# A four-layer state-space stack on one core: output scaling moved behind the projection, additions moved to identity matmuls and ScalarE copies

## The chip, the cores and the metric

The kernel runs on one core of a Trainium2 chip. The metric is the device time of one execution in microseconds (us). The engines are called PE (TensorE), DVE (VectorE), ACT (ScalarE), POOL (GpSimd) and SP (SyncE, which here issues every DMA). Each engine executes its own instructions in the order in which the program gives them, and waits at semaphores for the others.

## The reference

Eight images of 48 x 48 positions and 96 channels pass through four residual layers, `x = x + layer(groupnorm(x))`. Layers 0 and 3 are two-dimensional selective scans, layer 1 is a filtered expansion (upsampling, a polynomial, downsampling), and layer 2 is a selective scan along lines in four directions. What the change touches is the end of layers 0 and 3, and the end of layer 2:

```
# layers 0 and 3, y: sum of the four scans, 192 channels
mu = y.mean(-1); yc = y - mu; var = (yc * yc).mean(-1)
y = yc * rsqrt(var + 1e-5) * out_norm_w + out_norm_b
y = y * silu(z)
x = x + y @ out_proj_w.T                     # 192 -> 96 channels

# layer 2, one term for each direction k
x = x + (y_k * silu(z_k)) @ w_k ... + out_b
```

Everything is float32.

## The kernel before

The channels lie on the partitions and the positions along the free axis. The 192 inner channels are kept as two halves of 96. An image is cut into five blocks of positions (`BLKS`: four of 480 and one of 384).

`scans()` drives layers 0, 2 and 3. It goes over the images (jobs), the four directions and the five blocks, 160 blocks a layer. A block has four turns. A turn makes three scans on DVE (L263); each needs a pair of decays `ps_da` that ACT writes into PSUM (L255, two buffers), and products `dbu` that DVE and POOL make (L235). POOL then multiplies the scanned states by the C rows (L276), and PE sums them over the states (L296, L298). Where a block carries on from the one before it, ACT copies the carried state into `dbu` (`bring`, L243). Nothing is scheduled by a planner: the order on each engine is the order of the Python statements.

Each turn calls `aside()` twice. Such a call is a half-turn here. In this order, it loads data for the next block, advances the generator `side(job)` by one `yield`, runs a step of `stage1` (which prepares a block two blocks ahead), and runs what `later` holds. On DVE the first call of a turn falls before the third scan and the second one after it.

In layers 0 and 3 `side(job)` finishes the image before (`post`) and then prepares the next one (`front`, `conv`), beside the scans of the image in hand. For the last image `post` runs alone, after the last scan. `post` has two loops over the five blocks. The first subtracts the mean (L507), squares (L510) and sums to variances (L515). The second, in which a block takes five half-turns, is this:

- load the stored silu(z) (`zin`, one buffer) and the residual rows (`xi`, two buffers) by SP; spread the reciprocal deviations over the partitions by PE into `pr` (L534)
- DVE multiplies each half of `y` by `out_norm_w` and by `pr` (L538)
- POOL multiplies `y` by z (L541); PE starts the projection with the norm's bias, `wnb` times z (L544)
- PE adds the projection of `y` (L547)
- DVE adds the result to `xi` (L550), and SP stores it (L552) at the start of the next block's first half-turn

`pr`, `po` and all other PSUM tiles of the side work are one buffer, the tag "side". In `stage1` of these layers PE's projection `s0` (L593) stands in slot 0 of a block's eight half-turns, and ACT's copy of it (`bcl`, L598) in slot 1; `raw` (L583) on PE stands in slots 3 and 4, and `biased` (L587) on ACT in slots 4 and 5. These run after the side work of the same half-turn.

In layer 2 (`lines`) `done()` hands over a finished block: DVE multiplies by the gate (L785), one half-turn later `project()` lets PE project it into a PSUM tile of tag "s1" (two buffers, L794), and another half-turn later `add()` lets DVE add it to the image `xs` in place (L800 for direction 0, with the bias `l2_outb`; L802 for the others). For two directions the positions are taken by columns, so that the image is read and written with a step of 48 elements.

Of the kernel before, what the change touches and what calls it, by code (L numbers as in the profile page):

```python
# [9 lines left out]
F32 = mybir.dt.float32  # L10
AF = mybir.ActivationFunctionType
ALU = mybir.AluOpType
# [3 lines left out]
H, W, C = 48, 48, 96  # L16
L = H * W
DH = 96
# [7 lines left out]
BMAX = 480  # L26
# [49 lines left out]
def vss_stack_kernel(ctx: ExitStack, tc: tile.TileContext, i: dict, out: bass.AP):  # L76
    nc = tc.nc
# [19 lines left out]
    wc = weights(const, ("gmat", "ident", "red"))  # L97
# [332 lines left out]
    def ss2d(l, xin, xout, b0=0):  # L430
# [65 lines left out]
        def post(b):  # L496
            y = yss[b]
            var = small.tile([CH, L // CH], F32, tag="var", name="var")
            for r0, nr in BLKS:
                n = nr * SEG  # L500
                s = slice(r0 * W, r0 * W + n)
# [7 lines left out]
                sq = lnp.tile([DH, 2, BMAX], F32, tag="sq", name="sq", bufs=1)  # L509
# [14 lines left out]
            for r0, nr in BLKS:  # L524
                n = nr * SEG
                s = slice(r0 * W, r0 * W + n)
                z = lnp.tile([DH, 2, BMAX], F32, tag="zin", name="zin", bufs=1)
                nc.sync.dma_start(z[:, :, :n], zs[b][:, :, s])  # L528
                xi = xio.tile([C, BMAX], F32, tag="xi", name="xi")
                nc.sync.dma_start(xi[:, :n], xin[b][:, s])  # L530
                pr = side_psum()
                for c in range(n // CH):
                    at = r0 * W // CH + c
                    nc.tensor.matmul(pr[:DH, c * CH:(c + 1) * CH], lhsT=var[:, at:at + 1].to_broadcast([CH, DH]),  # L534
                                     rhs=wc["ident"], start=True, stop=True)
                yield
# [4 lines left out]
                nc.gpsimd.tensor_mul(y[:, :, s], y[:, :, s], z[:, :, :n])  # L541
                po = side_psum()
                for half in range(2):
                    nc.tensor.matmul(po[:C, :n], lhsT=wnb[:, half, :], rhs=z[:, half, :n], start=(half == 0), stop=False)  # L544
                yield
                for half in range(2):
                    nc.tensor.matmul(po[:C, :n], lhsT=w[f"{l}_out"][:, half, :], rhs=y[:, half, s],  # L547
                                     start=False, stop=(half == 1))
                yield
                nc.vector.tensor_add(xi[:, :n], xi[:, :n], po[:C, :n])  # L550
                yield
                nc.sync.dma_start(xout[b][:, s], xi[:, :n])  # L552

        def side(job):
# [82 lines left out]
        dirs = DIRS_SS  # L637
# [11 lines left out]
    def lines(xin, xout):  # L649
# [40 lines left out]
        xs = {}  # L690
# [90 lines left out]
        def done(b, half, y):  # L781
            n = b.n
            if half == 0:
                gated[b] = gp.tile([DH, 2, BMAX], F32, tag="gated", name="gated")
            nc.vector.tensor_mul(gated[b][:, half, :n], b.zb[:, half, :n], y[:DH, :n])  # L785
            if half == 0:
                return []
            got = {}

            def project():  # L790
                got["o"] = ps("s1", 2)
                t = gated.pop(b)
                for h in range(2):
                    nc.tensor.matmul(got["o"][:C, :n], lhsT=wo[:, b.k, h, :], rhs=t[:, h, :n], start=(h == 0), stop=(h == 1))  # L794

            def add():
                xv = seq(xs[b.job], dirs[b.k][0])[:, b.r0:b.r0 + b.nr, :]
                v = rows(got["o"][:C], n)
                if b.k == 0:
                    nc.vector.scalar_tensor_tensor(xv, v, w["l2_outb"], xv, ALU.add, ALU.add)  # L800
# [17 lines left out]
        dirs = DIRS_L2  # L818
# [293 lines left out]
```

## Time and profile before

| | us |
|---|---|
| median of 3 runs | 19549.3 (19545.86 to 19551.5) |
| profiled execution, its own time | 19542.61 |
| span of the profiled execution, first to last instruction | 19540.6 |

| engine | busy us | share of the span |
|---|---|---|
| DVE | 16831.8 | 86% |
| POOL | 16028.7 | 82% |
| PE | 15237.1 | 78% |
| ACT | 14144.5 | 72% |

From the start of the span to about 6008 us layer 0 runs, to about 7230 us layer 1, to about 13540 us layer 2, and then layer 3. The mean granted PE clock is 0.744 of full speed. A float32 matmul stands in the profile as two matmul instructions, so a count of x320 is 160 matmuls.

In a row of the timeline, the first number is the start in us from the start of the span, the second the length in us, then come the engine, the line, the operation, the tile written and the tiles read, and the shape. What stands in square brackets is the idle time of the engine just before, and who ended it. In a row of a group, the busy time and the mean in nanoseconds follow the first bar, and the idle time before the instructions the second.

### The profile page before, as it was taken

How to read it: one execution, taken by the hardware profiler on the slowest of the kernel's cores; microseconds unless marked ns; L12 is line 12 of the kernel's file. 1: busy time of each engine (PE TensorE's matmuls, PEld its weight loads, DVE VectorE, ACT ScalarE, POOL GpSimd, SP SyncE). 2: the span in 40 equal slices, each digit the busy share in tenths (PEclk: the TensorE clock that was granted, in tenths of full speed). 3: DMA queues.
4: the chain of work that ended last, by engine and by line, in shares of the span. 5: the costliest groups of instructions: out<-in, count | busy, mean ns of one | idle time of the engine just before them, and what ended most of it. 6: DMA issues, size and time to landing. Idle time of an engine off the chain costs nothing. (4 is left out here: it accounts for less than half of the span.)

```text
span 19540.6 us, 172984 instructions
## 1 busy us (share of the span) xinstructions
PE 15237.1 (78%) x53500; PEld 4370.8 (22%) x53500; DVE 16831.8 (86%) x11281; ACT 14144.5 (72%) x22222; POOL 16028.7 (82%) x9825
## 2 busy tenths in 40 slices
PE   6777777777767887888888988887677777777776
PEld 1211211211214552222222222222121121121121
DVE  6999999999992228999999999996999999999997
ACT  5877777877772227788788777885778778778775
POOL 6999999999991007888888888886999999999997
PEclk6777776776767777888878888887677677667765
DMA  3444444444443324434434444443444444444443
GB/s 130 160 162 158 162 160 163 158 163 158 156 170 48 50 45 145 145 141 150 150 139 147 147 146 145 144 149 112 158 163 160 159 164 157 160 162 161 156 165 123
DMA packets 768486, 2829.44 MB, mean 145 GB/s; under 512 B 235724, under 2 KB 298668, under 8 KB 640926
## 3 DMA queue, kind: packets, MB, share of 16 engines
q1 hardware_dynamic: 767558, 2818.38, 43.1%
q8 instruction: 422, 6.91, 0.1%
q14 instruction: 506, 4.15, 0.1%
HBM read 2371.42 MB, written 446.69 MB: 144 GB/s over the span
## 5 line engine op out<-in xcount | busy, mean ns | idle before, releaser
L263 DVE TENSOR_TENSOR_SCAN dbu<-ps_da,dbu 128x962 f32<-128x962 f32 (+3 forms) x5760 | 11858.2, 2071 | 897.9 <-ACT ps_da L255 895.7
L276 POOL TENSOR_TENSOR dbu<-dbu,bc 128x1440 f32<-128x1440 f32 (+1 forms) x3840 | 11439.8, 2985 | 1040.6 <-DVE dbu L263 814.0
L255 ACT ACTIVATE ps_da<-dd,w_l_a 128x481 f32<-128x481 f32 (+3 forms) x11520 | 7414.7, 648 | 2729.7 <-DVE dbu L263 2523.7
L296 PE MATMUL ps_y<-dbu,w_red 128*32 128x480 f32 (+1 forms) x23040 | 4983.6, 752 | 3051.0 <-POOL dbu L276 3047.3
L298 PE MATMUL ps_y<-dbu,w_red 128*32 128x480 f32 (+1 forms) x7680 | 4942.9, 752 | 0.0
L235 DVE TENSOR_TENSOR dbu<-dd,ps_b 128x1440 f32<-128x1440 f32 (+5 forms) x3840 | 4645.3, 1210 | 320.1 <-ACT ps_b L216 275.7
L235 POOL TENSOR_TENSOR dbu<-dd,bc 128x480 f32<-128x480 f32 (+3 forms) x1920 | 3026.2, 1576 | 61.9 <-DMA bc<-bcd 36.6
L296 PEld LDWEIGHTS ps_y<-dbu,w_red 128*32 128x32 f32 x23040 | 742.7, 125 | 7009.7 <-POOL dbu L276 5283.6
L216 ACT COPY ps_b<-bc 128x480 f32<-128x480 f32 (+1 forms) x3360 | 1798.4, 535 | 300.7 <-DVE dbu L235 271.3
L722 PE MATMUL ps_s<-xpad,w_l_cw 128*128 128x480 f32 (+1 forms) x2560 | 1747.2, 834 | 2.3 <-ACT xpad L124 1.6
L481 PE MATMUL ps_side<-xpad,w_l_cw 128*128 128x480 f32 (+1 forms) x2880 | 1617.4, 690 | 4.6 <-ACT xpad L124 4.5
L255 ACT ACT_TABLE_LOAD x970 | 1244.5, 1283 | 17.1
L113 POOL MEMSET w_l_cw<- 128x1760 f32 (+1 forms) x3 | 5.8, 1942 | 1326.7 <-DVE x L932 1321.3
L422 POOL TENSOR_TENSOR dds<-dds,u 96x480 f32<-96x480 f32 (+1 forms) x640 | 793.6, 1240 | 259.9 <-ACT dds L611 259.9
L593 PE MATMUL ps_s<-u,w_l_xp 96*38 96x480 f32 (+1 forms) x1280 | 957.2, 888 | 4.1 <-ACT dds L587 3.0
L583 PE MATMUL ps_s<-bcl,dtw 6*96 6x480 f32 (+1 forms) x1280 | 878.4, 775 | 86.3 <-ACT dds L587 82.2
L270 POOL COPY carry<-dbu 128x3 f32<-128x3 f32 x2048 | 386.4, 189 | 582.6 <-DVE dbu L263 570.2
L292 PE MATMUL ps_y<-ysum,w_ident 96*96 96x480 f32 (+1 forms) x960 | 740.7, 861 | 113.7 <-ACT ysum L634 112.8
L481 PEld LDWEIGHTS ps_side<-xpad,w_l_cw 128*128 128x128 f32 x2880 | 571.0, 222 | 1115.0 <-issue 916.4
L722 PEld LDWEIGHTS ps_s<-xpad,w_l_cw 128*128 128x128 f32 x2560 | 525.8, 210 | 1087.1 <-issue 938.1
L298 PEld LDWEIGHTS ps_y<-dbu,w_red 128*32 128x32 f32 x7680 | 683.1, 125 | 0.0
L763 PE MATMUL ps_s<-xpad,w_l_inz 96*96 96x480 f32 (+1 forms) x640 | 505.7, 924 | 86.9 <-ACT dds L757 69.2
(146 smaller groups left out, 12586.2 us busy)
## 6 DMA issues: line engine op xcount, KB each, us to landing
dd<-dd SPq DMA_DIRECT2D x512, 1443.0 KB
bc<-bcd SPq DMA_DIRECT2D x1536, 480.0 KB
dd<-dd SPq DMA_DIRECT2D x256, 1440.0 KB
dd<-dds SPq DMA_DIRECT2D x512, 360.8 KB
dd<-dd SPq DMA_DIRECT2D x128, 1155.0 KB
bc<-bcd SPq DMA_DIRECT2D x384, 384.0 KB
dd<-dds SPq DMA_DIRECT2D x256, 360.0 KB
dd<-dd SPq DMA_DIRECT2D x64, 1152.0 KB
```

The costliest lines, as they stand in the source:

```text
L216: nc.scalar.copy(bps[t][:, :b.n], bcs[t][:, 0, :b.n])
L235: engine.tensor_mul(o, du, by.unsqueeze(1).to_broadcast([P, hi - lo, b.n]))
L255: nc.scalar.activation(da[:, at:at + b.m], b.got[half][:, u % 3, 0, :], AF.Exp, scale=a[:, b.k, ci:ci + 1])
L263: nc.vector.tensor_tensor_scan(db, da, db, 0.0, ALU.mult, ALU.add)
L276: nc.gpsimd.tensor_mul(h, h, bcs.pop(2 * t + sub)[:, 1, :n].unsqueeze(1).to_broadcast([P, 3, n]))
L296: nc.tensor.matmul(y[32 * g:32 * g + 32, :n], lhsT=wc["red"][:, :32], rhs=hc[:, g, b.at], start=False, stop=(slot == 3))
L298: nc.tensor.matmul(y[DH:, :n], lhsT=wc["red"][:, 32:], rhs=hc[:, 2, b.at], start=(slot == 0), stop=(slot == 3))
L422: nc.gpsimd.tensor_mul(rows(du, n), rows(dt, n), u)
L481: nc.tensor.matmul(pu[:, :n], lhsT=flat[:, at:at + P], rhs=xpad[:, r0 + dy:r0 + dy + nr, dx:dx + W], start=(tap == 0), stop=(tap == 8))
L583: nc.tensor.matmul(got["p"][:DH, :n], lhsT=dtw[2 * NS:, b.k, half, :], rhs=b.bcl[2 * NS:, :n], start=True, stop=True)
L593: nc.tensor.matmul(got["p"][:NBC, :n], lhsT=w[f"{l}_xp"][:, b.k, half, :], rhs=u[:, half], start=(half == 0), stop=(half == 1))
L722: nc.tensor.matmul(got["u", half][:, :n], lhsT=flat[:, at:at + P], rhs=shifted(off), start=(tap == 0), stop=(tap == 3))
```

## The change

In layers 0 and 3 the weight `out_norm_w` is multiplied into the output projection's weights once, ahead of the loops. (The product of `out_norm_b` with the same weights, `wnb`, is made from the weights as they were.) The reciprocal deviation, which is the same for all channels of a position, is applied behind the projection. So POOL's multiplication of `y` by z moves ahead of it, into the half-turn in which z is loaded. ACT copies `pr` into SBUF, PE projects `y * z`, DVE multiplies the 96 projected channels by the copy, and PE gathers the result in a second PSUM tile: the residual rows and the scaled product by two products with the identity matrix, and the bias term by its two products with z. ACT copies the sum into `xi`. The copy and the store now stand in the half-turn after these four matmuls, which is the first one of the next block.

In layer 2 `project()` begins with a product of the identity and the image's own rows, and `add()` becomes a copy on ACT (with the bias for direction 0) in place of the addition on DVE.

```diff
         for half in range(2):
             nc.scalar.activation(wnb[:, half, :], w[f"{l}_out"][:, half, :], AF.Identity, scale=w[f"{l}_nb"][:, half:half + 1])
+            wo = w[f"{l}_out"][:, half, :]
+            nc.scalar.activation(wo, wo, AF.Identity, scale=w[f"{l}_nw"][:, half:half + 1])
...
                     nc.tensor.matmul(pr[:DH, c * CH:(c + 1) * CH], lhsT=var[:, at:at + 1].to_broadcast([CH, DH]),
                                      rhs=wc["ident"], start=True, stop=True)
-                yield
-                for half in range(2):
-                    nc.vector.scalar_tensor_tensor(y[:, half, s], y[:, half, s], w[f"{l}_nw"][:, half:half + 1], pr[:DH, :n],
-                                                   ALU.mult, ALU.mult)
-                yield
                 nc.gpsimd.tensor_mul(y[:, :, s], y[:, :, s], z[:, :, :n])
+                yield
+                t = lnp.tile([DH, 2, BMAX], F32, tag="sq", name="normed", bufs=1)[:, 0, :n]
+                nc.scalar.copy(t, pr[:DH, :n])
+                yield
                 po = side_psum()
                 for half in range(2):
-                    nc.tensor.matmul(po[:C, :n], lhsT=wnb[:, half, :], rhs=z[:, half, :n], start=(half == 0), stop=False)
-                yield
+                    nc.tensor.matmul(po[:C, :n], lhsT=w[f"{l}_out"][:, half, :], rhs=y[:, half, s],
+                                     start=(half == 0), stop=(half == 1))
+                yield
+                nc.vector.tensor_mul(t, t, po[:C, :n])
+                yield
+                po = side_psum()
+                nc.tensor.matmul(po[:C, :n], lhsT=wc["ident"], rhs=xi[:, :n], start=True, stop=False)
                 for half in range(2):
-                    nc.tensor.matmul(po[:C, :n], lhsT=w[f"{l}_out"][:, half, :], rhs=y[:, half, s],
-                                     start=False, stop=(half == 1))
-                yield
-                nc.vector.tensor_add(xi[:, :n], xi[:, :n], po[:C, :n])
-                yield
+                    nc.tensor.matmul(po[:C, :n], lhsT=wnb[:, half, :], rhs=z[:, half, :n], start=False, stop=False)
+                nc.tensor.matmul(po[:C, :n], lhsT=wc["ident"], rhs=t, start=False, stop=True)
+                yield
+                nc.scalar.copy(xi[:, :n], po[:C, :n])
                 nc.sync.dma_start(xout[b][:, s], xi[:, :n])
...
+            xv = seq(xs[b.job], dirs[b.k][0])[:, b.r0:b.r0 + b.nr, :]
             def project():
                 got["o"] = ps("s1", 2)
                 t = gated.pop(b)
+                nc.tensor.matmul(got["o"][:C, :n], lhsT=wc["ident"], rhs=xv, start=True, stop=False)
                 for h in range(2):
-                    nc.tensor.matmul(got["o"][:C, :n], lhsT=wo[:, b.k, h, :], rhs=t[:, h, :n], start=(h == 0), stop=(h == 1))
+                    nc.tensor.matmul(got["o"][:C, :n], lhsT=wo[:, b.k, h, :], rhs=t[:, h, :n], start=False, stop=(h == 1))
             def add():
-                xv = seq(xs[b.job], dirs[b.k][0])[:, b.r0:b.r0 + b.nr, :]
                 v = rows(got["o"][:C], n)
                 if b.k == 0:
-                    nc.vector.scalar_tensor_tensor(xv, v, w["l2_outb"], xv, ALU.add, ALU.add)
+                    nc.scalar.activation(xv, v, AF.Identity, bias=w["l2_outb"])
                 else:
-                    nc.vector.tensor_add(xv, xv, v)
+                    nc.scalar.copy(xv, v)
```

More of the change, by code (lines that the diff above doesn't have):

```diff
@@ L535, in post @@
                                      rhs=wc["ident"], start=True, stop=True)
+                nc.gpsimd.tensor_mul(y[:, :, s], y[:, :, s], z[:, :, :n])
                 yield
-                for half in range(2):
-                    nc.vector.scalar_tensor_tensor(y[:, half, s], y[:, half, s], w[f"{l}_nw"][:, half:half + 1], pr[:DH, :n],
-                                                   ALU.mult, ALU.mult)
+                t = lnp.tile([DH, 2, BMAX], F32, tag="sq", name="normed", bufs=1)[:, 0, :n]
+                nc.scalar.copy(t, pr[:DH, :n])
                 yield
-                nc.gpsimd.tensor_mul(y[:, :, s], y[:, :, s], z[:, :, :n])
                 po = side_psum()
                 for half in range(2):
-                    nc.tensor.matmul(po[:C, :n], lhsT=wnb[:, half, :], rhs=z[:, half, :n], start=(half == 0), stop=False)
+                    nc.tensor.matmul(po[:C, :n], lhsT=w[f"{l}_out"][:, half, :], rhs=y[:, half, s],
+                                     start=(half == 0), stop=(half == 1))
                 yield
+                nc.vector.tensor_mul(t, t, po[:C, :n])
+                yield
+                po = side_psum()
+                nc.tensor.matmul(po[:C, :n], lhsT=wc["ident"], rhs=xi[:, :n], start=True, stop=False)
                 for half in range(2):
-                    nc.tensor.matmul(po[:C, :n], lhsT=w[f"{l}_out"][:, half, :], rhs=y[:, half, s],
-                                     start=False, stop=(half == 1))
+                    nc.tensor.matmul(po[:C, :n], lhsT=wnb[:, half, :], rhs=z[:, half, :n], start=False, stop=False)
+                nc.tensor.matmul(po[:C, :n], lhsT=wc["ident"], rhs=t, start=False, stop=True)
                 yield
-                nc.vector.tensor_add(xi[:, :n], xi[:, :n], po[:C, :n])
-                yield
+                nc.scalar.copy(xi[:, :n], po[:C, :n])
                 nc.sync.dma_start(xout[b][:, s], xi[:, :n])
```

## The prediction

> **What bounds the kernel now.** I read the page's busy shares and costliest groups first, then the busy time by stage, then the timeline of one image around each line that the change touches.
>
> ```profile
> span 19540.6 us, 172984 instructions
> PE 15237.1 (78%) x53500; PEld 4370.8 (22%) x53500; DVE 16831.8 (86%) x11281; ACT 14144.5 (72%) x22222; POOL 16028.7 (82%) x9825
> L263 DVE TENSOR_TENSOR_SCAN dbu<-ps_da,dbu 128x962 f32<-128x962 f32 (+3 forms) x5760 | 11858.2, 2071 | 897.9 <-ACT ps_da L255 895.7
> ```
>
> By stage (columns: window, its length, busy PE, PEld, DVE, ACT, POOL, granted clock, DMA share, GB/s):
>
> ```profile
> 145.00:5904.00 5759.00, 4262.70 (x14982) 1048.40 (x14986) 5430.73 (x3472) 4441.45 (x7258) 5306.44 (x3612) 0.70 0.47 160
> 5904.00:6008.00 104.00, 70.33 (x220) 35.69 (x212) 16.27 (x26) 7.40 (x8) 13.37 (x6) 0.61 0.10 28
> 7230.00:13540.00 6310.00, 5310.73 (x16532) 1425.48 (x16530) 5663.41 (x3813) 4927.42 (x7151) 5375.64 (x2567) 0.81 0.40 143
> ```
>
> In the first ss2d layer DVE is busy 94% and POOL 92%; in the line layer DVE 90%, POOL 85%, PE 84%, ACT 78%. DVE leads, but every engine is in a loop with it: a scan needs the decays (ps_da) from ACT, two buffers deep; ACT takes its copies in order and some wait for PE; PE waits for POOL's products. Freed DVE time counts only as far as the decays are ready, and a late POOL comes back round. From 5904 to 6008 no scans run: the last image's post() is a bare chain (it recurs in the last 107 us), and all that lengthens it is paid.
>
> **What the Trainium skill says.** "ScalarE: Activation LUTs", Table sets: copy and identity are in every set. Agreed: none of the trace's table loads stands on the Identity of L587 or the copies of L634, so the new copies bring none. "DMA: Bandwidth & Descriptors", Latency: about 2 us of fixed cost. Here z needs 4.4 us from issue to its use in the bare chain. "SBUF — State Buffer", Who interferes with whom: a DVE instruction with one SBUF input does not contend with GpSimd. The removed DVE operations read one from SBUF and one from PSUM, so POOL should not speed up; its 96x960 product takes 2.20 us in the bare chain with DVE idle, 2.22 among the scans: agreed. "TensorE: Matmul & The Clock Gate", HAM oscillation: PE after idle gaps runs at half clock. Agreed: two 480-column matmuls (four instructions) take 3.5 us or 1.8 us.
>
> **The change, part by part.** Call the steps of a post() block A to E, one to each half-turn, and F the end, which falls into the next block's A.
>
> *DVE.* Removed by their groups: L538 102.5, L550 50.1, L800 27.5, L802 102.5 = 282.6 us. Added: 80 products of L550's shape, 50.1. Net -232.5 us. DVE also waited for PE before these (14.9 + 110.2 + 33.1 + 82.9 = 241 us); those waits move to ACT, which now reads the results.
>
> *ACT.* 160 copies in post at 0.55 (0.47 for the short block): 85 us. 160 in the line layer: 80 in row order at 0.55 to 0.65, 80 in column order at 0.97 (L634's column rows): 125 us. Four small weight scalings: 1 us, before the loop.
>
> *PE.* 160 identity matmuls in post and 160 in lines. L544 and L547 give 428.2/320 = 1.34 us a matmul, L794 423.1/320 = 1.32: 426 us, beside other work except where named below.
>
> *Lines.* In one block (DVE, then ACT):
>
> ```profile
> 9026.64 2.15 DVE L263 TENSOR_TENSOR_SCAN dbu<-ps_da,dbu 128x960 f32<-128x960 f32 x1
> 9029.07 0.71 DVE L800 SCALAR_TENSOR_TENSOR x<-ps_s,w_l_outb,x 96x480 f32<-96x480 f32 x1 [0.28 <-PE ps_s L794]
> 9029.71 2.14 DVE L263 TENSOR_TENSOR_SCAN dbu<-ps_da,dbu 128x960 f32<-128x960 f32 x1
> ```
>
> ```profile
> 9027.86 1.36 ACT L255 ACTIVATE ps_da<-dd,w_l_a 128x480 f32<-128x480 f32 x2
> 9029.64 1.35 ACT L255 ACTIVATE ps_da<-dd,w_l_a 128x480 f32<-128x480 f32 x2
> ```
>
> Without the addition the scan of 9029.71 could start at 9029.25, when its decays are ready: gain 0.45, not 0.99. The same two limits at 159 blocks give 146 us. But ACT's copy now waits for a project() one matmul longer (mean 1.1 us there) and delays the next decays. Taking from each block's slack this wait and a copy of 0.55 or 0.95 us leaves 90 or 60 us. I take **-75 us**; ends -146 (ACT's wait costs nothing) and -20 (the longer PE queue delays decays again later).
>
> *Last post(), twice.* Before, a block takes 11.4 us (from the end of one addition, 5975.87, to the next, 5987.25); z's load covers the norm's work and is itself exposed:
>
> ```profile
> 5976.37 0.56 SPq L528 DMA_DIRECT2D zin<-zd  x1
> 5980.80 2.20 POOL L541 TENSOR_TENSOR ysum<-ysum,zin 96x960 f32<-96x960 f32 x1 [10.07 <-DMA zin<-zd]
> 5984.05 2.52 PE L547 MATMUL ps_side<-ysum,w_l_out 96*96 96x480 f32 x4
> 5986.60 0.65 DVE L550 TENSOR_TENSOR xi<-xi,ps_side 96x480 f32<-96x480 f32 x1 [7.40 <-PE ps_side L547]
> ```
>
> After: 0.5 to the issue of z, 4.4 to POOL, 2.2 product, two matmuls 2.7 (between 1.8 and 3.5), DVE product 0.7, then four matmuls 5.4 (3.7 to 7.0), which all stand behind that product because "side" has one PSUM buffer, ACT copy 0.55 and handovers 0.25: 16.7. Four intervals of 43.5 us become 64 (the last shorter), +21; the first block, whose z is there, +3. Twice 24 = **+48 us** (25 to 68 by PE's clock).
>
> *Post beside the scans, 14 images.* The moved step is POOL's y*z (L541): from two half-turns after z's load to the same half-turn. And SP issues z later: behind the store of xi, which waits for ACT's copy in F, after four matmuls, instead of the DVE addition in E. The second block of an image:
>
> ```profile
> 15273.84 0.62 SPq L528 DMA_DIRECT2D zin<-zd  x1
> 15275.14 2.49 POOL L276 TENSOR_TENSOR dbu<-dbu,bc 128x1152 f32<-128x1152 f32 x1 [0.71 <-DVE dbu L263]
> 15277.58 1.68 POOL L235 TENSOR_TENSOR dbu<-dd,bc 128x768 f32<-128x768 f32 x1
> 15282.02 2.22 POOL L541 TENSOR_TENSOR ysum<-ysum,zin 96x960 f32<-96x960 f32 x1
> 15280.16 0.20 ACT L243 COPY dbu<-carry 128x6 f32<-128x6 f32 x1 [1.09 <-DVE dbu L235]
> ```
>
> POOL's new place is before 15275.14. E's four matmuls start once the reductions are done, about 15272, and end at 15276.7 to 15278.5; ACT's copy ends 0.6 later, z is issued 0.4 after that and is usable 4.4 later: 15282.1 to 15283.9. POOL, ready at about 15275, stalls 7 to 9 us, with L276, the products of L235, and PE's reductions queued behind it. In the built program that turn's carry copy on ACT (L243) waits for POOL's L235, and the decays of the next scans stand behind L243. It waits for L235 in few turns, but here it does. L235 would end near 15289, not 15279.27; slack is 0.9 to L243 and 1.5 from the decays to their scan: DVE loses about 6 us. The fourth block has the same short way from E to F, without that carry wait: ACT held about 2 us and raw(1) behind the four matmuls, 3.5 in all. In the third and fifth E is early and POOL waits some 4 us; about 2 each reach DVE. The first block's z comes at once; it and the final F cost 1.5. Together +15 an image. Against it: two L538 take 1.25 us (15279.99 to 15281.24), of which 0.6 is free of decays, times 5 = 3; the addition with its PE wait (0.5 + 0.5) less the new product, 2.5; L547 no longer ahead of s0 in one turn, 1.5. Net +8 an image, **+112 us** (-70 to +224).
>
> *Sum.* -75 + 48 + 112 = **+85 us** on the profiled execution's 19542.6 (span 19540.6 and 2.0 around it). The median of the three runs is 6.7 higher at 19549.3, so I carry the difference over: about **19635 us**.
>
> **The rivals.**
> (a) *Faster: POOL's stall stays covered.* Most carry copies do not wait for L235, and POOL's products are consumed a turn later. The mechanism: less work on DVE, with POOL's late product eating its lead only. It decides once the second block's stall is under 0.9 + 1.5 = 2.4 us, or DVE is late anyway there. Then an image gains 3 + 2.5 + 1.5 less 2 for ACT's waits, -5 x 14 = -70; with -75 and +48: -97, 19452 us. For it: DVE's 94%, and the 4.4 us DVE stall just before (decays behind bcl), in which POOL could catch up. Against: POOL's 92% and the moved wait.
> (b) *No change*: an image costs +2 (+28), lines -75, last posts +48: 19550 us.
> (c) *PE and ACT bound the posts too*: an image +16 (+224), lines -40, +48: 19781 us. For it: ACT waits already up to 5.8 us for PE at bcl; against: PE is idle, waiting for POOL, thousands of us in all.
>
> **How the numbers follow.** Forecast 0.51, (a) 0.25, (b) 0.12, (c) 0.12. Faster or slower means by over 0.2% (39 us), about what a measurement of this kernel can tell from no change. The forecast and (c) are slower: 0.63. The forecast's own range is 19590 to 19710; the whole range, from (a)'s centre with its spread to (c)'s, is 19440 to 19790.
>
> **What would show it.** Right: POOL's y*z released by the DMA of z about 70 times, not 8; the last posts some 24 us longer each; the line stage 75 us shorter; the ss2d stages 50 us longer each in spite of less DVE work; ACT idle behind PE at the new copies. Wrong: ss2d stages shorter, or POOL's wait for z below 2 us a block. Line stages longer would mean that ACT's in-order wait, not DVE's addition, sets the pace there.

## The result, and the profile after

The changed kernel takes 19972.7 us (median of 4 runs, 19970.3 to 19991.0) against 19547.6 us before (4 runs, 19542.4 to 19551.5): ratio 1.022, 95% interval 1.0202 to 1.0237. It is slower, by 425 us. The prediction had the direction right, but gave 19635 us and a range that ends at 19790.

The page of the changed kernel, the lines that answer to those shown of before:

```profile
span 19970.4 us, 174280 instructions
PE 15533.7 (78%) x54140; PEld 4481.0 (22%) x54140; DVE 16637.7 (83%) x10961; ACT 14287.0 (72%) x22546; POOL 16013.9 (80%) x9825
L263 DVE TENSOR_TENSOR_SCAN dbu<-ps_da,dbu 128x962 f32<-128x962 f32 (+3 forms) x5760 | 11848.1, 2068 | 1187.6 <-ACT ps_da L255 1186.3
```

VectorE works 194 us less than before (16637.7 against 16831.8) and yet the span grew by 430 us. The scans themselves cost the same (2068 ns each, before 2071), but their idle time ahead rose from 897.9 to 1187.6 us, nearly all of it put down to decays that ScalarE had not yet made.

By stage (window, length, busy PE, PEld, DVE, ACT, POOL, granted clock, DMA share, GB/s), the first ss2d layer, its last post(), and the line layer:

```profile
145.00:6058.00 5913.00, 4321.68 (x15118) 1061.59 (x15118) 5392.47 (x3402) 4464.33 (x7328) 5298.97 (x3611) 0.70 0.46 156
6058.00:6197.00 139.00, 87.44 (x240) 40.80 (x240) 10.54 (x21) 12.79 (x18) 14.51 (x7) 0.60 0.10 26
7429.00:13784.00 6355.00, 5424.11 (x16851) 1484.08 (x16849) 5559.49 (x3653) 5010.52 (x7312) 5373.56 (x2567) 0.82 0.41 142
```

In the ss2d layer DVE is busy 91% (5392.47 of 5913; before 94%) and POOL 90% (before 92%): everyone waits more. From the first scan to the last, the two ss2d layers grew by 154.9 and 152.4 us, the line layer by 45.4 us; the last post() by 31.7 us. The first image of each ss2d layer, which has no post() beside it, is unchanged (about 705 us); each of the others takes about 22 us more (in the middle of a layer about 747 us in place of 725).

The second ss2d layer in the list of waits (who waits for whom: us in total, times, longest):

```profile
POOL ysum L539 <- DMA zin<-zd: 156.2, 35, 6.8
DVE normed L549 <- PE ps_side L546: 134.4, 21, 8.2
ACT dbu L243 <- POOL dbu L235: 90.2, 19, 7.8
```

Before, POOL has no wait for z there; the wait of DVE's addition for its projection and that of the carry copies are these:

```profile
DVE xi L550 <- PE ps_side L547: 19.3, 9, 2.8
ACT dbu L243 <- POOL dbu L235: 24.2, 12, 2.4
```

POOL waits for z in all 35 blocks of that layer's seven posts, 4.5 us each on average; by the place of the block in its image, 1.3, 6.3, 5.6, 5.2 and 4.0 us. The other two lines are what the wait looks like further on. In the second block of one image (z's load on SP, POOL's product, the carry copy on ACT, the next scan on DVE):

```profile
15544.06 0.62 SPq L531 DMA_DIRECT2D zin<-zd  x1
15548.45 2.20 POOL L539 TENSOR_TENSOR ysum<-ysum,zin 96x960 f32<-96x960 f32 x1 [5.46 <-DMA zin<-zd]
15553.05 1.67 POOL L235 TENSOR_TENSOR dbu<-dd,bc 128x768 f32<-128x768 f32 x1
15554.75 0.20 ACT L243 COPY dbu<-carry 128x6 f32<-128x6 f32 x1 [7.24 <-POOL dbu L235]
15556.09 1.76 DVE L263 TENSOR_TENSOR_SCAN dbu<-ps_da,dbu 128x770 f32<-128x770 f32 x1 [6.35 <-ACT ps_da L255]
```

The start times of the scans, set against those of the kernel before at the same place of an image (median over six images), step up three times, by 7 to 8 us each: at the second block, the third and the fifth. From there on they stay at 22. The fourth block, priced at 3.5, adds nothing, although POOL waits 5.2 us for z in it. The second block is the predicted sequence, in the predicted place: 4.4 us from z's issue to its use, the carry copy behind POOL's L235, and DVE idle 6.35 us where the prediction said about 6. (POOL's own wait was shorter than the 7 to 9 us predicted: 5.46 here, 6.3 on average.) The third block of the same image was priced at about 2 us; DVE idles 8.15 us in it:

```profile
15570.54 0.61 SPq L531 DMA_DIRECT2D zin<-zd  x1
15575.23 2.22 POOL L539 TENSOR_TENSOR ysum<-ysum,zin 96x960 f32<-96x960 f32 x1 [5.81 <-DMA zin<-zd]
15579.09 2.90 POOL L276 TENSOR_TENSOR dbu<-dbu,bc 128x1440 f32<-128x1440 f32 x1
15582.05 1.02 PE L296 MATMUL ps_y<-dbu,w_red 128*32 128x480 f32 x3 [5.15 <-POOL dbu L276]
15587.08 3.52 PE L546 MATMUL ps_side<-ysum,w_l_out 96*96 96x480 f32 x4
15590.64 0.65 DVE L549 TENSOR_TENSOR normed<-normed,ps_side 96x480 f32<-96x480 f32 x1 [8.15 <-PE ps_side L546]
```

POOL is late for L276, PE's reductions are late for it, the projection L546 stands behind the reductions, and DVE's new product, which stands ahead of the next scan, waits 8.15 us for the projection.

The last post() of the kernel, one block on the chain that ended last (start, length):

```profile
19914.93 4.25 DMA zin<-zd
19919.22 0.09 issue
19919.31 2.21 POOL ysum L539
19921.52 0.04 issue
19921.57 3.53 PE ps_side L546 x4
```

Then, after DVE's product:

```profile
19925.89 1.91 PE ps_side L552 x2
19927.81 3.20 PE ps_side L554 x4
19931.01 1.61 PE ps_side L555 x2
```

The predicted chain, link for link: z's load, POOL, projection, product, four matmuls. From one product of POOL to the next the blocks take 17.5, 19.0 and 17.5 us, not 16.7: the projection took 3.53 us where the sum had 2.7, and the four matmuls up to 6.7 where it had 5.4. PE waits 5.2 to 6.3 us before each of these projections, and then runs two 480-column matmuls in 3.5 us instead of the 1.8 of the prediction's shorter case. The Trainium skill ("TensorE: Matmul & The Clock Gate", HAM oscillation) says so of PE after idle gaps, and this trace agrees.

### The profile page after: what moved, and what is told of

It reads as the page before. It is cut to its first block, busy times and chain, and to the rows that moved or that the text cites. A ratio compares the mean times of both kernels' runs of the same rounds, so it can differ in the third digit from the quotient of the medians.

```text
span 19970.4 us, 174280 instructions
## 1 busy us (share of the span) xinstructions
PE 15533.7 (78%) x54140; PEld 4481.0 (22%) x54140; DVE 16637.7 (83%) x10961; ACT 14287.0 (72%) x22546; POOL 16013.9 (80%) x9825
## 4 chain that ended last, share of the span: by engine, by line
DVE 26%; PE 22%; POOL 17%; ACT 15%; issue 12%; DMA 7%; SPq 0%; POOLq 0%; DVEq 0%; ACTq 0%
DVE dbu L263 16%; POOL dbu L276 13%; DVE dbu L235 9%; ACT ps_da L255 5%; PE ps_s L728 3%; PE ps_y L296 3%; ACT L255 3%; DMA dd<-dd 2%; POOL dds L422 2%; PE ps_h L961 2%; PE ps_side L484 2%; DMA dd<-dds 2%; POOL dbu L235 2%; PE ps_y L974 1%; PE ps_s L599 1%
## 5 line engine op out<-in xcount | busy, mean ns | idle before, releaser
L263 DVE TENSOR_TENSOR_SCAN dbu<-ps_da,dbu 128x962 f32<-128x962 f32 (+3 forms) x5760 | 11848.1, 2068 | 1187.6 <-ACT ps_da L255 1186.3
L276 POOL TENSOR_TENSOR dbu<-dbu,bc 128x1440 f32<-128x1440 f32 (+1 forms) x3840 | 11431.7, 2983 | 1107.5 <-DVE dbu L263 884.0
L296 PE MATMUL ps_y<-dbu,w_red 128*32 128x480 f32 (+1 forms) x23040 | 4924.7, 745 | 3212.7 <-POOL dbu L276 3209.7
L235 DVE TENSOR_TENSOR dbu<-dd,ps_b 128x1440 f32<-128x1440 f32 (+5 forms) x3840 | 4633.9, 1207 | 318.0 <-ACT ps_b L216 276.6
L298 PE MATMUL ps_y<-dbu,w_red 128*32 128x480 f32 (+1 forms) x7680 | 4882.7, 745 | 0.0
L235 POOL TENSOR_TENSOR dbu<-dd,bc 128x480 f32<-128x480 f32 (+3 forms) x1920 | 3022.2, 1574 | 64.8 <-DMA bc<-bcd 37.0
L255 ACT ACT_TABLE_LOAD x970 | 1244.5, 1283 | 17.5
```

What stands on the lines that cost most here:

```text
L235: engine.tensor_mul(o, du, by.unsqueeze(1).to_broadcast([P, hi - lo, b.n]))
L255: nc.scalar.activation(da[:, at:at + b.m], b.got[half][:, u % 3, 0, :], AF.Exp, scale=a[:, b.k, ci:ci + 1])
L263: nc.vector.tensor_tensor_scan(db, da, db, 0.0, ALU.mult, ALU.add)
L276: nc.gpsimd.tensor_mul(h, h, bcs.pop(2 * t + sub)[:, 1, :n].unsqueeze(1).to_broadcast([P, 3, n]))
L296: nc.tensor.matmul(y[32 * g:32 * g + 32, :n], lhsT=wc["red"][:, :32], rhs=hc[:, g, b.at], start=False, stop=(slot == 3))
L298: nc.tensor.matmul(y[DH:, :n], lhsT=wc["red"][:, 32:], rhs=hc[:, 2, b.at], start=(slot == 0), stop=(slot == 3))
```

## The experiments

All comparisons are with the kernel before, run on the same chip in the same batch. The last columns come from each profiled run: what the scans of the two ss2d layers, those of the line layer, and the last post() took more than before. Where a kernel leaves the line layer as it was, its scans still differ by -20 to +3 us from before, and the stage between the first ss2d layer and the line layer, less that layer's last post(), by -4 to +32 us: differences of this size in those two places are not read as effects.

| kernel | ratio (95% interval) | us | ss2d scans | line scans | last post |
|---|---|---|---|---|---|
| changed kernel | 1.0220 (1.0202 to 1.0237) | +425 | +155, +152 | +45 | +32 |
| lines_only | 1.0027 (1.0016 to 1.0037) | +54 | +3, 0 | +48 | 0 |
| post_only | 1.0188 (1.0173 to 1.0204) | +369 | +151, +150 | -13 | +29 |
| post_ident | 1.0008 (1.0000 to 1.0016) | +13 | +3, +8 | -20 | +4 |
| z_ahead | 1.0030 (1.0020 to 1.0041) | +62 | +24, +17 | -20 | +11 |
| lines_pe | 1.0089 (1.0074 to 1.0105) | +176 | +6, 0 | +154 | 0 |
| lines_noid | 0.9965 (0.9952 to 0.9977) | -72 | +6, +4 | -69 | 0 |
| lines_rows | 1.0001 (0.9993 to 1.0009) | -3 | +6, -1 | -10 | 0 |
| d_late | 1.0190 (1.0176 to 1.0204) | +372 | +155, +151 | -16 | +27 |
| pool_no_z | 1.0022 (1.0015 to 1.0028) | +40 | +23, +13 | -18 | +9 |
| mul_late | 1.0081 (1.0065 to 1.0096) | +157 | +51, +40 | +1 | +29 |
| post_shift | 1.0164 (1.0150 to 1.0178) | +326 | +131, +142 | 0 | +31 |
| before_z_ahead | 0.9992 (0.9985 to 0.9999) | -15 | +4, +1 | -10 | -5 |
| pool_more | 1.0017 (1.0009 to 1.0025) | +34 | +23, +20 | -7 | +2 |
| before_gate_dve | 1.0037 (1.0024 to 1.0049) | +67 | +43, +36 | +3 | +2 |
| gate_dve | 1.0058 (1.0045 to 1.0070) | +104 | +47, +57 | -10 | +7 |
| pool_no_z_long | 1.0118 (1.0101 to 1.0135) | +236 | +110, +106 | -6 | +12 |

### Which part costs what

*lines_only*: the diff's last hunk alone, on the kernel before.

> Only the line layer is changed (identity product and ScalarE copy in project() and add()); post() is as before. Theory 1 (the parts act apart from each other, and the line layer's loss is real): the scans of the line layer take 45 us more than before, the two ss2d layers do not move, whole time +40 to +60 us. Rival (the prediction's working: DVE's freed time counts in the line layer; the loss seen there in the changed kernel comes over from the posts): -75 us (-146 to -20).

*post_only*: the diff without its last hunk.

> Only post() and its weights are changed; the line layer is as before. Theory 1 (parts act apart): +150 us in the scans of each ss2d layer, +32 us in each last post, together +360 to +385 us. Rival (prediction's working): +160 us.

54 + 369 = 423 us, and the whole change 425: the parts add up. Both lost more than the prediction's working gave them (-75 and +160).

*post_ident*: only the residual and the copy in post(), in the old order of steps.

```
                 po = side_psum()
+                nc.tensor.matmul(po[:C, :n], lhsT=wc["ident"], rhs=xi[:, :n], start=True, stop=False)
...
-                nc.vector.tensor_add(xi[:, :n], xi[:, :n], po[:C, :n])
+                nc.scalar.copy(xi[:, :n], po[:C, :n])
```

> One part of the change to post() alone: the residual by an identity product ahead of the weighted z's products in the one po tile, and a ScalarE copy in place of the DVE addition; the norm's scale, its weights and the order of the other steps stay as before. Theory 1 (the loss of the posts comes from POOL's product moved up to z's load and from DVE's product between two PE steps, not from the residual's two instructions of PE): an image of the ss2d stages moves by -4 to +2 us, whole time -60 to +30 us. Rival (PE's longer queue makes reductions and scores late): +5 to +10 us an image, +70 to +140 us.

+13 us, at the edge of what can be told from nothing (an image moves by 2.6/7 and 8.2/7, about +1 us). The identity product and the addition taken off DVE together come to about nothing. Whether neither does anything, or a gain and a loss cancel, this run cannot tell. The loss of 22 us an image comes with the reordering around the norm's scale.

### What in post() costs 22 us an image

*z_ahead*: post_only, with z loaded a block ahead into a second buffer (and the residual rows a half-turn later, into one buffer).

```
+            def load_z(n):
+                r0, nr = BLKS[n]
+                z = lnp.tile([DH, 2, BMAX], F32, tag="zin", name="zin", bufs=2)
+                nc.sync.dma_start(z[:, :, :nr * SEG], zs[b][:, :, r0 * W:r0 * W + nr * SEG])
+                return z
...
+                z = ahead
+                if nblk + 1 < len(BLKS):
+                    ahead = load_z(nblk + 1)
```

> post() and weights as changed, line layer as before, but z of a block is loaded one block ahead into a second buffer (xi then has one buffer and is loaded one half-turn later). Theory 1 (POOL's wait for z starts both losses: the carry copy behind POOL in the second block, and in the third and fifth DVE's product, which stands in DVE's order for a projection that stands on PE behind reductions that wait for the late POOL): an image of the ss2d stages comes from +22 down to +4 us or less, each last post loses 4.5 us a block, 18 us: whole time +40 to +90 us against before. Rival 2 (DVE's product waits because it stands one scan after its projection, whatever POOL does): only the second block's 7 us go, 15 us an image stay: +210 to +250 us.

*pool_no_z*: post_only, with one operand of POOL's product changed, so that the gate z is left out of it.

```
-                nc.gpsimd.tensor_mul(y[:, :, s], y[:, :, s], z[:, :, :n])
+                nc.gpsimd.tensor_mul(y[:, :, s], y[:, :, s], y[:, :, s])
```

> post() and weights as changed, line layer as before, every load, store and buffer as changed; only POOL's product takes y times y in place of y times z, so the gate is left out of the projected term and nothing of POOL waits for z in step A. This takes away POOL's wait for the transfer and nothing else (the run with z a block ahead also moved a load and split buffers). Theory 1 (POOL's wait for z is the root of the whole loss beside the scans, the product's new place alone costs little): an image of the ss2d stages +2 to +5 us in place of +22; each last post about 32 - 4 x 4.9 = +12 us; whole time +50 to +110 us. Rival (the product's place before the turn's other POOL work, or the later PE steps, cost by themselves): +12 us an image or more, +200 us or more.

Both bring an image from +22 down to between +2.5 and +3 us (23.5 + 17.1 us over fourteen images; 22.8 + 12.6). The two runs get rid of the wait by different means, and each has a side effect of its own: z_ahead moves another load, and POOL's product is 0.4 us shorter in pool_no_z. As they agree, POOL's wait for z is the root of almost the whole loss. In the list of waits of the second ss2d layer in pool_no_z, POOL no longer waits for z, and the other two have shrunk with it, from the 130 and 90 us of post_only to 25 and 27:

```profile
ACT dbu L243 <- POOL dbu L235: 27.3, 13, 2.4
DVE normed L549 <- PE ps_side L546: 24.9, 15, 2.7
```

So far the two consequences (carry copy, DVE's product) look like the two paths by which the wait reaches the scans. The next two runs were to remove one each.

*d_late*: post_only, one more `yield` between the projection and DVE's product.

> post() and weights as changed, line layer as before; one empty half-turn is put between the projection (C) and DVE's product (D). z's load and POOL's product stay where the change put them, so POOL still waits for z. Theory 1 (in the third and fifth block the loss is DVE's product waiting in DVE's order for a projection one scan earlier): DVE's waits for the projection go, an image of the ss2d stages loses +6 to +12 us, about the second block's share, in place of +22; whole time +150 to +250 us against before. Rival (POOL's stall itself reaches DVE through the decays and carry copies, and DVE's wait is only where it shows): +20 us or more an image stay, +340 us or more.

*post_shift*: post_only, `range(4)` for `range(3)` ahead of post() in side().

> post() and weights as changed, line layer as before; the whole of post() starts one half-turn later, so that the first, third and fifth block start A where the second and fourth did. If the loss of a block depends on its half-turn as the prediction has it (a carry copy on ScalarE waits for POOL's late product only where A stands in the odd half-turn), the third and fifth block now lose by the carry copy and the second and fourth by DVE's product, four losses of 7 to 8 us in place of three: +27 to +31 us an image, whole time +440 to +510 us. If any late POOL product costs the same wherever it falls: +20 to +24 us an image, +340 to +400 us.

In its total d_late answers as the rival had it: 151 us in the second ss2d layer, as much as without the empty half-turn. The list of waits of that layer shows the product's wait as good as gone (7.5 us of formerly 130) and the loss unmoved, for the scans now wait for their decays (476.7 us; 376.6 in post_only):

```profile
DVE dbu L263 <- ACT ps_da L255: 476.7, 324, 6.9
POOL ysum L539 <- DMA zin<-zd: 122.2, 35, 7.0
ACT dbu L243 <- POOL dbu L235: 50.0, 18, 4.3
DVE normed L550 <- PE ps_side L546: 7.5, 7, 1.6
```

But d_late takes away more than that one wait. A block now takes six half-turns in place of five, so the second to fifth block come one to four half-turns later, z's load and POOL's product with them, against what the expectation says; the loss steps up at other scans than in post_only. The run shows that the loss does not hang on DVE's place behind the projection alone; it does not show by what path the scans lose there.

And post_shift, which was to turn two losses into carry-copy losses, came out at +19 to +20 us an image and +326 in all. That rules out the four losses of the first answer, and is a little under the range of "any late POOL product costs the same wherever it falls"; its carry copies wait for POOL's L235 only 40.6 us (89.5 in post_only). In both runs one of the two visible paths shrank and the loss hardly moved, so neither path alone is its cause. That the late POOL reaches DVE by whatever way is open fits this, but no run shows the ways one by one.

*mul_late*: post_only, with POOL's product behind the first `yield` (step B).

> post() and weights as changed, line layer as before; POOL's product moves one half-turn behind z's load, into step B, which is one half-turn before the projection that needs it. Theory 1: most of POOL's wait for z is gone (a half-turn is about 4.4 us, the transfer 4.4 to 7), the product is still ready for the projection; an image +3 to +10 us, whole time +100 to +200 us; last posts unchanged at +30 each. Rival (the projection now waits for POOL on PE and DVE's product behind it, so the loss moves there): +18 us an image or more, +310 us or more.

+157 us: the scans of the two layers lose 91 us in place of 301. POOL still waits 32.1 us for z in that layer, and the layer is 39.9 us longer.

### How much of POOL's time at that place is paid

By now a pattern stood out in the second ss2d layer: POOL's waits for z of 156.2, 152.1, 147.6, 32.1 and 9.9 us (changed kernel, post_only, post_shift, mul_late, z_ahead) go with losses of 152.4, 149.9, 142.3, 39.9 and 17.1 us. d_late does not fit (122.2 us of waits, 151.1 lost). Yet DVE is the busier engine. Is POOL itself out of slack there?

*pool_more*: before, with a product that nobody needs in each step A.

```
+            spare = lnp.tile([DH, 2, BMAX], F32, tag="sq", name="spare", bufs=1)
+            nc.gpsimd.memset(spare, 1.0)
             for r0, nr in BLKS:
...
+                nc.gpsimd.tensor_mul(spare[:, :, :n], spare[:, :, :n], spare[:, :, :n])
```

> The kernel before with one more POOL product of the gate's size (96x960, 2.2 us, on a spare tile that nobody waits for, and nothing is waited for) at the start of each block's step A, so that POOL's busy time grows by about 11 us an image beside the scans. Theory N (POOL has no slack in the stretch of the posts: its time is paid one for one whether it stalls or works): +8 to +12 us an image, whole time +120 to +190 us. Theory S (POOL has slack for work, and a stall cost its full length because it came at a bad place in the order): 0 to +3 us an image, 0 to +50 us.

*before_gate_dve*: before, `nc.vector.tensor_mul` for `nc.gpsimd.tensor_mul` in y times z.

> The kernel before with one word changed: post()'s product of y and z on VectorE in place of POOL. DVE gets about 1.05 us more a block (5 us an image), POOL loses 2.2 us a block (11 us an image). Theory N: an image gains 4 to 10 us, -60 to -140 us. Theory S (DVE is the bound, POOL has slack): +3 to +6 us an image, +40 to +90 us; the last posts gain 1 us a block either way, -8 to -10 us.

*gate_dve*: the same word in z_ahead.

> The kernel with z one block ahead, changed post() and old line layer, with the product of y and z on VectorE in place of POOL; z is there, so nothing waits for a transfer. Against the run with z ahead DVE has 5 us more an image, POOL 11 us less. Theory N: 5 to 10 us an image less than with z ahead, -30 to -90 us against before, the fastest so far. Theory S: 3 to 6 us an image more than with z ahead, +100 to +150 us against before.

All three speak for Theory S. POOL does have slack for work: 9.5 us more an image cost 3. DVE has little: before_gate_dve gives it the product and loses 5.6 us an image, though POOL is relieved of 10.7. The size of the DVE product was wrong in the expectation, which had 1.05 us (before_gate_dve; minimum, median and maximum in ns):

```profile
L541 DVE TENSOR_TENSOR ysum<-ysum,zin x80: 954/1514/3597, 1008.3 to 19617.6; 96x960 f32<-96x960 f32 x64, 96x768 f32<-96x768 f32 x16
```

In gate_dve, where it stands in step A, its median is 3.08 us. The Trainium skill ("SBUF — State Buffer", Who interferes with whom) says that a DVE instruction with two SBUF inputs contends with a GpSimd instruction that reads SBUF; both inputs of this product are in SBUF, and the trace of before_gate_dve agrees: its 96x960 products take 1.15 us where no POOL instruction runs beside them (8 of 64), and 1.13 to 3.28 us where one does.

*pool_no_z_long*: pool_no_z, with the product of y and y issued three times in a row.

> As the run without z in POOL's product (the gate is left out of the projected term), but with the product of y and y issued three times in a row in step A, so that POOL is busy there 5.3 us a block, about as long as wait and product together took (6.5 us), and waits for nothing. Theory L (POOL's time at this place counts, wait or work alike: free up to about 2 us, paid beyond): the 17 us more an image cost 10 to 16 us, and the last posts 17 us each: +220 to +310 us against before. Rival W (the wait is special; work costs the 0.3 us for each us that the added products cost): 4 to 6 us an image, +110 to +180 us.

Theory L: +236 us with no wait for a transfer at all, and the start times step up at the same three places as in the changed kernel (second, third and fifth block, by 4 to 6 us each). Over the 35 blocks of the second ss2d layer, POOL's time in the moved step (wait, from the list of waits, and product, from its mean over four 480-column blocks and a short one) against the layer's loss, per block:

| kernel | wait + product, us | loss, us |
|---|---|---|
| pool_no_z | 0 + 1.72 | 0.36 |
| z_ahead | 0.28 + 2.13 | 0.49 |
| mul_late | 0.92 + 2.13 | 1.14 |
| pool_no_z_long | 0 + 5.15 | 3.02 |
| post_shift | 4.22 + 2.13 | 4.07 |
| post_only | 4.35 + 2.13 | 4.28 |

Wait or work, these six lie on one curve: little is paid up to about 2 us; from 1.72 to 5.15 us 0.78 is paid for each us, from 5.15 to 6.48 us 0.95. (A straight line from mul_late to post_shift, both with waits, has 3.0 us at 5.15; the run without a wait lost 3.02.) d_late lies above it (5.62 us, loss 4.32), with its blocks at other places; why was not tried. And the curve is one of averages over the five blocks: in the changed kernel the fourth block's 5.2 us of wait cost nothing, and the third's and fifth's cost more than their length. What decides that from block to block stays open.

### What in the line layer costs 50 us

*lines_pe*: before, with only the identity product added, as a group of its own that the projection overwrites.

```
+                nc.tensor.matmul(got["o"][:C, :n], lhsT=wc["ident"], rhs=xv, start=True, stop=True)
```

> PE's cost of the line layer's change by itself: the identity product of x is issued in project() as a group of its own ahead of the projection, which overwrites it; the DVE additions stay as before, so DVE gets no relief and ScalarE no copy. Theory PE (the loss of the line layer comes from two more matmul instructions ahead of each projection, behind which the reductions and so the gated products on DVE come late): the line layer's scans take 40 to 75 us more than before. Theory ACT (it comes from ScalarE's copies and their in-order wait for PE): 0 to +15 us.

*lines_noid*: before, with only the additions replaced by ScalarE copies, so that the residual is left out.

> ScalarE's cost by itself: the DVE additions are replaced by ScalarE copies as in the changed kernel, without the identity product, so the residual of the line layer is left out of the computation. Theory PE: the line layer gains what the prediction gave it without the longer PE queue, -100 to -40 us. Theory ACT: it loses as much as the whole change does there, +30 to +60 us, most of it in the two column directions where a copy takes 0.99 us.

Both runs fall on the side of Theory PE, lines_pe beyond its range. DVE's relief and ScalarE's copies together gain 72 us. lines_only is lines_noid with the identity product, and loses 54: on top of the copies, the product costs 126 us. In lines_noid (the page) DVE works 108 us less than before:

```profile
PE 15253.0 (78%) x53500; PEld 4391.3 (23%) x53500; DVE 16723.4 (86%) x11121; ACT 14227.9 (73%) x22382; POOL 16018.8 (82%) x9825
```

The 176 us of lines_pe are not the product's price in the changed kernel. In lines_pe DVE still adds, and in the list of waits from 7400 to 13400 us its additions of k = 1 to 3 wait 201.4 us for PE, in before 80.0; the gated products, which the theory named, wait 32.2 us, in before 28.4. The changed kernel has no such additions.

```profile
DVE x L804 <- PE ps_s L796: 201.4, 91, 3.3
```

What carries the 126 us can be read from the same window in lines_noid, and then in lines_only:

```profile
DVE gated L785 <- PE ps_y L298: 75.0, 73, 2.8
DVE dbu L263 <- ACT ps_da L255: 385.5, 468, 3.3
ACT x L802 <- PE ps_s L794: 10.2, 23, 0.8
```

```profile
DVE gated L785 <- PE ps_y L298: 151.6, 94, 3.1
DVE dbu L263 <- ACT ps_da L255: 421.9, 518, 3.3
ACT x L805 <- PE ps_s L798: 113.8, 89, 2.2
```

With the identity product, DVE's gated products wait 77 us longer for PE's reductions, and its scans 36 us longer for their decays; ACT's copies, which stand ahead of decays, wait 114 us for the projection in place of 10. So PE's queue reaches DVE in two ways, through the reductions and through ACT. The first is the larger by these waits; no run takes away one of the two alone.

*lines_rows*: lines_only for k = 0 and 1 alone.

> The line layer's change in the two row directions alone (k = 0, 1); the column directions keep their DVE additions, post() is as before. In the changed kernel an image gains up to 3.6 us by the middle of the row directions, is 2.3 to 2.7 us ahead at their end, and loses it again in the column directions. If the loss belongs to the column directions (strided reads and writes), this kernel is 10 to 30 us faster than before; if the loss is a debt of the row directions paid later, it is 0 to +50 us.

-3 us (-14 to +18 by the interval): between the two answers. In the row directions relief and longer PE queue about cancel; by subtraction, the loss of lines_only belongs to the column directions. Why there was not tried: a 96x480 ScalarE copy takes longer in them (about 1.0 us against 0.55), but so does the DVE addition that it replaces (1.01 against 0.65).

In the changed kernel PE's queue is seen at the block that the prediction read for its gain:

```profile
9231.02 1.05 PE L802 MATMUL ps_s<-x,w_ident 96*96 96x480 f32 x2
9231.91 1.77 PE L804 MATMUL ps_s<-gated,wo 96*96 96x480 f32 x4
9233.52 2.75 PE L728 MATMUL ps_s<-xpad,w_l_cw 128*128 128x384 f32 x8
```

```profile
9231.52 2.15 DVE L263 TENSOR_TENSOR_SCAN dbu<-ps_da,dbu 128x960 f32<-128x960 f32 x1
9234.14 2.16 DVE L263 TENSOR_TENSOR_SCAN dbu<-ps_da,dbu 128x960 f32<-128x960 f32 x1 [0.46 <-ACT ps_da L255]
```

Here the gain is there: 2.62 us from scan to scan, before 3.07, the predicted 0.45. But the identity product (median 0.99 us an instruction, two a block) stands ahead of the projection, of the next block's convolution and of the reductions, and in other turns the gated products on DVE wait for those, the 151.6 us above.

### A version that is faster than both

*before_z_ahead*: the kernel before, with the load of z_ahead and nothing else.

> The kernel before with only z's load moved one block ahead (two z buffers, one xi buffer, xi loaded a half-turn later). Beside the scans POOL's product comes two half-turns after z's load already, so nothing is to be had there: 0 (-20 to +20 us). In each last post z's exposed part goes: z's products on PE and POOL's product start 1.5 us earlier, the projection follows POOL's product without PE still working on z: 2 to 2.5 us a block, 8 to 10 us a post: -16 to -20 us in all, about 0.1%, a version that would beat both kernels by little. Rival (the store and load of the one xi buffer take it back): 0 or slower.

19537.9 us against 19552.9, ratio 0.9992 (0.9985 to 0.9999): the only version that leaves nothing out and beats both kernels, by 15 us, which the interval barely parts from nothing. In the trace the last post is 4.8 us shorter, half of what was expected; two such posts explain some 10 of the 15 us, and the rest is no more than the scatter between stages that this kernel leaves alone.

## Why the prediction was wrong, and what it had right

**Right.** The direction and its cause: POOL's y times z, moved to z's load, waits for z ("POOL's y*z released by the DMA of z about 70 times": 78 in the whole run), and the ss2d stages grow in spite of less DVE work. The second block's loss was right in place and path, and near in size (DVE idle 6.35 us for about 6). The last posts were +29 to +32 instead of +24 each; the term that was too small is PE's speed after its idle gaps (3.53 for 2.7 us, up to 6.7 for 5.4).

**Wrong, the posts (+112 predicted, about +301 measured in the scans of post_only).** Two terms failed.

- "In the third and fifth E is early and POOL waits some 4 us; about 2 each reach DVE." The waits were near (5.3 and 3.9 us on average in post_only); what reached DVE was 7 to 8 us each. Of a wait of 4 the prediction let the slack (2.4 us in its reading of the second block) take about 2. By pool_no_z_long and the table, the wait and the moved product draw on one slack of some 2 us, and the product alone takes 2.1: nothing was left to cover the wait. The fourth block, priced at 3.5, cost nothing; so the sum is nearer than its terms, by luck. Together the waits cost 19 us an image (post_only less pool_no_z: 151.4 + 149.9 - 22.8 - 12.6 = 266 over fourteen), where the sum had 15.
- "two L538 ... 3, the addition with its PE wait ... 2.5, L547 no longer ahead of s0 ... 1.5": of the 7 us an image that these were to save, nothing is left on balance. With the wait gone (pool_no_z, z_ahead) an image still costs 2.5 to 3 us more than before. This is the larger miss: 9.5 us an image, 133 us in all, against 4 us an image, 56 in all, for the waits. How much of it is saving that never came, and how much the price of the product's new place, is open: post_ident, which takes the addition off DVE but adds an identity product, gains nothing, and no run removed the two L538 or moved L547 alone.

**Wrong, the lines (-75 predicted, +54 measured in lines_only).** The failing step is the pricing of the line layer's identity products as "beside other work except where named below"; below, only ACT's wait for them was named. They cost 126 us (lines_only less lines_noid). By the lists of waits the larger way is the one that was not named, PE's reductions behind them and DVE's gated products behind those (77 us more), and the smaller one is ACT's (36 us more ahead of the scans). ACT's wait itself was priced well: 1.1 us a copy on average, and measured about 0.9 (113.8 us for k = 1 to 3 and 32.3 for k = 0 in the window). That lines_noid has -72 and the prediction -75 is chance: the -75 already had that wait taken off, which lines_noid does not have. The prediction's own sentence for longer line stages, "ACT's in-order wait, not DVE's addition, sets the pace there", thus names one of two ways, and the smaller one.

**Wrong, the range.** The rival with more loss (c) named the engines' queues ("PE and ACT bound the posts too") but gave the lines still -40 and an image +16; none of the cases had the lines longer, though that was listed among what could be seen. With the lines at +54 and the posts at +15 an image without savings (+210 + 48), the sum would have been +312, and with the measured waits of 19 and rest of 2.5, +301 + 60 + 54 = +415.

Open: which turn-by-turn path carries the loss in d_late and post_shift, where neither the carry copy nor DVE's product accounts for it; why the fourth block costs nothing; and the 20 to 30 us by which stages that a kernel does not touch differ from before.

## What to carry to other kernels

When a product is moved up to its operand's load, add the transfer's wait and the product's own time before setting any slack against them; here, on the average of five blocks, some 2 us were free and 0.8 to 0.95 of the rest was paid. Rearranging what stands further down (d_late) gained nothing, while removing the first wait (pool_no_z, z_ahead) gained almost everything. Work taken off the busiest engine is worth what a run with only that part shows: in the line layer it was worth 72 us, and the two "hidden" matmul instructions a block that replaced it, on a PE busy 84% of that layer, cost 126.

## What the runs showed of the hardware that was not expected

POOL's 96x960 product takes 1.78 us when both operands and the result are one tile (y times y, in pool_no_z) and 2.21 us with y and z in two tiles:

```profile
L539 POOL TENSOR_TENSOR ysum<-ysum x80: 1457/1782/1807, 997.6 to 19521.3; 96x960 f32<-96x960 f32 x64, 96x768 f32<-96x768 f32 x16
```

The same product of y and z on DVE takes 1.15 us with no POOL instruction beside it and up to 3.28 us with one (before_gate_dve; up to 3.81 in gate_dve). A kernel that moves work from POOL to DVE should price it with POOL running.
